# A four-layer kernel on one core: an input request moved ahead, a third buffer at the end, and a normalisation moved from VectorE to ScalarE

## The chip, the cores and the metric

The kernel runs on one core of a Trainium2 chip. The metric is device time in microseconds. The engines are TensorE (PE in the profile; its weight loads are PEld), VectorE (DVE), ScalarE (ACT), GpSimd (POOL) and SyncE (SP), which here only issues DMAs. Each engine runs its own instructions in order and waits on semaphores for others. A DMA is issued by an engine's queue and carried out by sixteen DMA engines.

## The reference

The input is x of shape (16, 192, 64, 64) in float32. Four layers follow, each of the form x = x + layer(group_norm(x)), with 32 groups:

- layer 0 passes each value, less and plus one half, through a small per-channel network of tanh and linear maps; the difference of two sigmoids is a likelihood.
- layer 1 is a 1x1 convolution over the image and its four shifts by one pixel.
- layer 2 is a selective scan. The image is read in four orders (by rows, by columns, and both backwards). For each order, channel and each of 16 states:

```
dA = exp(delta * A)
h  = dA * h + (delta * u) * B
y  = sum over the 16 states of h * C
```

- layer 3 sums four depthwise convolutions (3x3, 5x5, 1x7, 7x1), mixes channels by a 1x1 convolution z, normalises z over the whole batch and clips it to 0..6.

Since layer 3's statistics run over all 16 images, its last step can only be done when z is known for all of them.

## The kernel before, in words

Two images form a pair: 384 channels are three tiles of 128 partitions (NT = 3) with 4096 pixels. There are eight pairs. `front` computes layers 0 and 1 and layer 2's projections of a pair; `scans` computes layer 2; `layer3` the convolutions and z, which goes to memory. `pair` calls `scans` and `layer3` in turn. The front of the next pair is a Python generator that `scans` advances by pieces between its own steps, so that its work lies among the scan's on every engine. Only the first pair's front runs alone, and the last pair's scans have no front beside them.

**Scans.** For each tile j, each order k and each chunk m of 1024 pixels there is a block t (48 blocks), and in it one step for each of the 16 states n (768 steps s). A step has: a broadcast load cb of a row of C (SP, two steps ahead), `spread` of B by PE into PSUM (two steps ahead), `decay` (ACT exponent, three steps ahead), `product` (DVE), `scan` (DVE, then ACT copies the last column to `state`, then POOL multiplies h by cb; at n % 4 == 1 a POOL DMA adds the neighbour's h), and `add_up` by PE four steps later, which sums h in PSUM. There are eight h buffers. The scans' instructions go through `_Engines(tc, True)`, so they stay in program order; everything made with `_Engines(tc, False)` or with `nc` directly is placed by the planner, which takes an instruction when its inputs and buffers are free in its own account of time.

Once per block, `step_rest` makes the next block's delta (n == 4, with two table loads on ACT) and du (POOL; n == 8). Once per tile, `load_xn` requests the next tile of x at step 14 of the last block but one (block 14 or 30), and `norm_xn` normalises it at step 5 of the last block (15 or 31). There is one xn buffer, so the request waits until the last du has read it.

**Layer 3 and `begin`.** `begin` prepares the first block of the next pair: it loads xn, dt and bp, normalises xn on DVE, and makes delta and du. `layer3` calls it before its third quarter (c == 2).

**The end.** With the batch statistics loaded (zs) and turned into a scale and a shift, 24 tiles are read back (zl from SP, rl, the layer's own input, from ACT's queue), finished by one ACT and one DVE instruction of 4096 columns, and stored from SP. zl and rl have two buffers each.

Of the kernel before, what the change touches and what calls it, by code (L numbers as in the profile page):

```python
# [11 lines left out]
F32 = mybir.dt.float32  # L12
BF16 = mybir.dt.bfloat16
AF = mybir.ActivationFunctionType
# [8 lines left out]
P = 128  # L23
C = 192
NT = 3
# [11 lines left out]
K, N, R = 4, 16, 6  # L37
LC = 1024
# [68 lines left out]
def conv_preact_kernel(ctx: ExitStack, tc: tile.TileContext, a: dict):  # L107
# [737 lines left out]
        E.table(SOFTPLUS)  # L845
        E.act.activation(delta, v, AF.Softplus, bias=dtb[:, k, j : j + 1])

    def begin(o, psum):


        E = _Engines(tc, False)
        k = ORDER[0]
        xn = over.tile([P, L], F32, name="xn")
        nc.sync.dma_start(out=xn, in_=row_tiles(o.x2)[:, 0, :])
        dt = load_dt(nc.sync, o, k, 0)
        bp = load_bp(nc.sync, o, k, 0)
        normalise(nc.vector, xn, xn, o.gm, o.rstd, 0)
        delta = over.tile([P, LC], F32, name="delta", tag="delta", bufs=2)
        make_delta(E, psum(), delta, dt, k, 0)
        du = over.tile([P, LC], F32, name="du", tag="du", bufs=2)  # L860
        nc.gpsimd.tensor_tensor(image(du), image(delta), columns(xn)[:, : LC // HW, :], ALU.mult)
        return xn, bp, delta, du

    def scans(i, o, p3, st3, begun, nxt):

        E = _Engines(tc, True)
        with ExitStack() as es:
# [43 lines left out]
                    xns[j] = over.tile([P, L], F32, name="xn")  # L911
                    E.sp.dma_start(out=xns[j], in_=row_tiles(o.x2)[:, j, :])

            def norm_xn(j):
                if j < NT:
                    normalise(E.dve, xns[j], xns[j], o.gm, o.rstd, j)

            def load_xc(t):
                if t < T and todo[t][1] == 0:
# [148 lines left out]
            for s in range(total):  # L1068
                t, n = divmod(s, N)
                j, k, at, first = todo[t]  # L1070
                if s + 2 < total:
                    load_c(s + 2)
                if n == 2:
                    next_bp(t + 1)
                if n == 4:
                    next_dt(t + 2)
                if n == 6:
                    load_xc(t + 1)
                product(s)
                E.between()  # L1080
                scan(s)


                if n == 4:
                    gstep = step_rest(t + 1) if t + 1 < T else iter(())
                    next(gstep, None)
                if s + 3 < total:
                    decay(s + 3)
                if s + 2 < total:
                    spread(s + 2)  # L1090
                if (t + 2) % (K * NC_) == 0 and n == 14:
                    load_xn(j + 1)
                if (t + 1) % (K * NC_) == 0 and n == 5:
                    norm_xn(j + 1)
                if n > 4:
                    next(fin, None)
                if t == T - 1 and n > 2:
                    next(gn0, None)
                if n == 3:
                    add_up(s - LATE)  # L1100
                    if s >= LATE and (s - LATE + 1) % (K * NC_ * N) == 0:
                        fin = finish(j - 1)
                elif n == 8:
                    next(gstep, None)

                if kind == "l0":
                    for _ in range({5: 0}.get(n, 1)):
                        kind = next(fr, None) if kind == "l0" else kind
                elif n != 5:
                    done = 0  # L1110
                    while done < (1.99 if n in (0, 8, 12) else 0.99) and kind != "l0":
                        kind = next(fr, 1)
                        done += kind if isinstance(kind, float) else 1
                if n != 3:
                    add_up(s - LATE)
# [10 lines left out]
    def layer3(i, st3, less0, rstd0, o_next):  # L1126
        E = _Engines(tc, False)

        with tc.tile_pool(name="l3s", bufs=1) as stat, tc.tile_pool(name="l3z", bufs=2) as zk, tc.tile_pool(
# [14 lines left out]
                on_scalar(E, v, v, less0, rstd0, 0)  # L1144
            pw = load("pw", [P, len(BLOCKS), P], w_)
            nc.sync.dma_start(out=x3_d[i, NT - 1], in_=X)
            gm = stat.tile([P, NT], F32, name="gm")
            rstd = stat.tile([P, NT], F32, name="rstd")
            banks = lambda name: pz.tile([P, 512], F32, name=name, tag="ps")
# [13 lines left out]
            begun = None  # L1163
            for c in range(4):
                if c == 2 and o_next is not None:
                    begun = begin(o_next, lambda: pt.tile([P, 1024], F32, name="l3_p"))
                ys = []
                for j in range(NT):

                    g = wk.tile([P, 1024], F32, name="l3_g")  # L1170
                    for tap in TAPS[PE_TAPS:own]:
                        first = tap is TAPS[PE_TAPS]
                        m = g if first else wk.tile([P, 1024], F32, name="l3_m", bufs=3)
                        nc.scalar.activation(  # L1174
                            image(m), window(j, 16 * c, 16, tap), AF.Copy, scale=factor(j, tap)
                        )
                        if not first:
                            nc.gpsimd.tensor_tensor(g, g, m, ALU.add)  # L1178
                    ps = pt.tile([P, 1024], F32, name="l3_p")
                    for h in range(2):  # L1180
                        cs = slice(512 * h, 512 * h + 512)
                        for t, tap in enumerate(TAPS[:PE_TAPS]):
                            nc.tensor.matmul(  # L1183
                                ps[:, cs],
                                diag[:, j, t, :],
                                window(j, 16 * c + 8 * h, 8, tap),
                                start=(t == 0),
                                stop=False,
                            )
                    for half in range(2):  # L1190
                        for r in range(2):
                            rows = slice(64 * r, 64 * r + 64)
                            h = (half + r) % 2
                            cs = slice(512 * h, 512 * h + 512)
                            nc.tensor.matmul(  # L1195
                                ps[rows, cs], ident[rows, rows], g[rows, cs], start=False, stop=True
                            )

                    y = wk.tile([P, 1024], F32, name="l3_y", tag=f"l3_y{j}")
                    for tap in TAPS[own:]:  # L1200
                        nc.vector.scalar_tensor_tensor(  # L1201
                            image(y if tap is TAPS[-1] else ps),
                            window(j, 16 * c, 16, tap),
                            factor(j, tap),
                            image(ps),
                            ALU.mult,
                            ALU.add,
                        )
                    ys.append(y)
                for jo in range(NT):  # L1210
                    z = zk.tile([P, 1024], F32, name="z")
                    for h in range(2):
                        ps = pz.tile([P, 512], F32, name="zp", tag="ps")
                        for n, (b, ji) in enumerate(INTO[jo]):
                            nc.tensor.matmul(  # L1215
                                ps,
                                pw[:, b, :],
                                ys[ji][:, 512 * h : 512 * h + 512],
                                start=(n == 0),
                                stop=(n == len(INTO[jo]) - 1),  # L1220
                            )
                        nc.scalar.copy(z[:, 512 * h : 512 * h + 512], ps)
                        nc.vector.bn_stats(zst[:, jo, 2 * c + h, :], z[:, 512 * h : 512 * h + 512])
                    nc.sync.dma_start(
                        out=row_tiles(z_d[i])[:, jo, 1024 * c : 1024 * c + 1024], in_=z
                    )
# [15 lines left out]
        for _ in front(0, sets[0], _Engines(tc, False), Banks(ps, 8), True):  # L1242
            pass
    with tc.tile_pool(name="b_ps", bufs=1, space=PSUM) as ps:
        begun = begin(sets[0], lambda: ps.tile([P, LC], F32, name="b_v"))
    for i in range(npair):
        begun = pair(i, i % 2, i + 1 if i + 1 < npair else None, begun)

# [1 line left out]
    with tc.tile_pool(name="fin", bufs=1) as fin, tc.tile_pool(  # L1250
# [42 lines left out]
        nc.vector.tensor_tensor(shift, mean, scale, ALU.mult)  # L1293
        nc.vector.tensor_tensor(shift, beta, shift, ALU.subtract)

        with tc.tile_pool(name="last", bufs=2) as lp:
            for i in range(npair):
                for j in range(NT):
                    z = lp.tile([P, L], F32, name="zl")
                    r = lp.tile([P, S, S], F32, name="rl")  # L1300
                    nc.sync.dma_start(out=z, in_=row_tiles(z_d[i])[:, j, :])
                    nc.scalar.dma_start(out=r, in_=x3_d[i, j])
                    nc.scalar.activation(  # L1303
                        z, z, AF.Relu, bias=shift[:, j : j + 1], scale=scale[:, j : j + 1]
                    )
                    nc.vector.scalar_tensor_tensor(  # L1306
                        image(z), image(z), 6.0, r[:, inside, inside], ALU.min, ALU.add
                    )
                    nc.sync.dma_start(out=row_tiles(out[i])[:, j, :], in_=z)
# [107 lines left out]
```

## Time and profile before

| | us |
|---|---|
| median of 3 runs | 27652.14 (27644.76 to 27657.57) |
| profiled execution | 27649.24 |
| its span | 27647.5 |
| DVE busy | 23966.9 (87%) |
| PE busy | 23437.4 (85%) |
| POOL busy | 20728.4 (75%) |
| ACT busy | 16170.9 (58%) |

The first pair's scans lie between 1202 and 4120 us of the span, its layer 3 between 4120 and 4460; each later pair repeats this. The end begins at about 27180. Busy shares are averages over these unlike stages. Two helpers record most instructions under one line (L66 for all that is kept in order), so groups are told apart by the tiles that they write and read. "Idle before" in a group is the time in which the engine stood still just ahead of it, and the name after it is what ended that. Idle time of an engine that isn't the one others wait for costs nothing.

### The profile page before, as it was taken

To read this page: it belongs to the slowest core of one execution; us is meant where nothing else is said; L and a number is where in the kernel's file an instruction comes from. 1 tells how busy PE (TensorE), PEld (TensorE's weight loads), DVE (VectorE), ACT (ScalarE), POOL (GpSimd) and SP (SyncE) were. 2 spreads that over 40 slices of the span, in tenths; PEclk is the share of its full clock that TensorE was granted. 3 is DMA by queue.
4 is the path that set the end of the run, shared out by engine and by line. 5 is a ranking of instruction groups with operands and counts; after the bars stand their busy time and mean duration, and the time that the engine had idled before them with its cause. 6 is when DMAs were issued, how large, how long until landed. Compare 5 with 4: busy or idle time off the path is not lost. (4 is left out here: it accounts for less than half of the span.)

```text
span 27647.5 us, 208708 instructions
## 1 busy us (share of the span) xinstructions
PE 23437.4 (85%) x57652; PEld 9614.6 (35%) x57652; DVE 23966.9 (87%) x15146; ACT 16170.9 (58%) x23198; POOL 20728.4 (75%) x10386
## 2 busy tenths in 40 slices
PE   8799978999789987999779997899978998776672
PEld 4343323433233332433334332333323333222221
DVE  0399988999899998999989998899989999899994
ACT  7388455874468644885548844587447855444442
POOL 2388877887778876888768887788777887677771
PEclk9899989999899998999889998999989999888886
DMA  4489874898568973898748986589747897367755
GB/s 102 135 224 228 222 213 137 226 223 223 156 193 227 226 225 119 226 226 224 218 128 226 226 219 191 157 227 223 226 133 213 225 224 226 113 189 194 198 163 243
DMA packets 1999218, 5471.76 MB, mean 198 GB/s; under 512 B 550440, under 2 KB 550664, under 8 KB 1977568
## 3 DMA queue, kind: packets, MB, share of 16 engines
q1 hardware_dynamic: 1773408, 4592.80, 56.4%
q0 software_dynamic: 221184, 805.40, 15.3%
q10 hardware_dynamic: 3456, 60.21, 0.6%
q8 instruction: 459, 7.52, 0.1%
q14 instruction: 711, 5.82, 0.1%
HBM read 3908.47 MB, written 340.96 MB: 154 GB/s over the span
## 5 line engine op out<-in xcount | busy, mean ns | idle before, releaser
L66 POOL TENSOR_TENSOR h<-h,cb 128x1024 f32<-128x1024 f32 x6144 | 14878.4, 2479 | 4244.1 <-ACT state L66 3331.4
L66 DVE TENSOR_TENSOR_SCAN h<-dA,state,pbt 128x1024 f32<-128x1024 f32 x4608 | 10809.2, 2346 | 736.2 <-ACT dA L66 106.0
L66 PE MATMUL ysum<-h,ident 128*128 128x512 f32 x18432 | 9427.6, 637 | 191.3 <-DMA h<-h 188.6
L66 DVE TENSOR_TENSOR pbt<-du,pbt 128x1024 f32<-128x1024 f32 x6144 | 7427.4, 1209 | 592.2 <-PE pbt L66 444.7
L66 ACT ACTIVATE dA<-delta,t_alog 128x1024 f32<-128x1024 f32 x6144 | 7042.4, 1148 | 6.5
L66 PEld LDWEIGHTS ysum<-h,ident 128*128 128x128 f32 x18432 | 3765.1, 205 | 4487.1 <-issue 3914.3
L66 ACT COPY state<-h 128x1 f32<-128x1 f32 x6144 | 1144.3, 186 | 6214.0 <-DVE h L66 6193.5
L66 PE MATMUL pbt<-bp,pick 96*128 96x512 bf16 x8192 | 2695.6, 414 | 1929.7 <-DVE h L66 1917.8
L66 DVE TENSOR_TENSOR_SCAN h<-dA,pbt 128x1024 f32<-128x1024 f32 x1536 | 3507.8, 2284 | 203.1 <-ACT dA L66 33.1
L66 PE MATMUL p<-t,wts 96*128 96x512 f32 x5376 | 2688.7, 598 | 122.0 <-ACT t L66 121.5
L66 PE MATMUL p<-m,wms 128*96 128x512 f32 (+1 forms) x5376 | 2658.9, 596 | 9.0 <-ACT t L66 5.3
L66 ACT ACTIVATE t<-p,bias 96x512 f32<-96x512 f32 x2688 | 1803.1, 678 | 914.5 <-PE p L66 901.9
L66 PEld LDWEIGHTS <-pick 96*128 96x128 bf16 x8192 | 697.3, 101 | 4716.9 <-DVE h L66 3101.5
L1178 POOL TENSOR_TENSOR l_g<-l_g,l_m 128x1024 f32<-128x1024 f32 x672 | 1614.5, 2404 | 633.5 <-ACT l_g L1174 455.6
L66 PE MATMUL l_p<-l_xp,w1s 128*128 128x512 f32 x3920 | 1840.3, 598 | 17.0 <-POOL l_xp L66 17.0
L66 PE MATMUL pbt<-bp,pick_mix 96*128 96x512 bf16 x4096 | 1283.6, 396 | 541.6 <-DVE h L66 535.7
L66 POOL DMA_DIRECT2D h<-h x1536 | 1365.5, 889 | 495.9 <-POOL h L66 421.5
L66 PEld LDWEIGHTS p<-t,wts 96*128 96x128 f32 x5376 | 1010.7, 190 | 1259.2 <-issue 890.5
L66 ACT ACT_TABLE_LOAD x1082 | 1388.2, 1283 | 19.2
L66 PEld LDWEIGHTS p<-m,wms 128*96 128x96 f32 (+1 forms) x5376 | 946.8, 177 | 746.3 <-issue 363.8
L1201 DVE SCALAR_TENSOR_TENSOR l_p<-xp,wc,l_p 128x1024 f32<-128x1024 f32 x768 | 985.6, 1289 | 244.5 <-PE l_p L1195 220.7
L66 ACT ACTIVATE m<-m,bias,sp 96x512 f32<-96x512 f32 x1344 | 1078.0, 803 | 174.0 <-DMA m<-l_xn 157.9
(242 smaller groups left out, 18743.2 us busy)
## 6 DMA issues: line engine op xcount, KB each, us to landing
cb<-cp_d SPq DMA_DIRECT2D x2048, 512.0 KB
cb<-c_d SPq DMA_DIRECT2D x2048, 512.0 KB
h<-h POOLq DMA_DIRECT2D x1536, 512.0 KB, 7.0
cb<-cp_d SPq DMA_DIRECT2D x2048, 256.0 KB
cb<-c_d SPq DMA_DIRECT2D x2048, 256.0 KB
m<-l_xn SPq DMA_DIRECT2D x3072, 128.0 KB
bp<-bp_d SPq DMA_DIRECT2D x384, 192.0 KB
x_d<-X SPq DMA_DIRECT2D x24, 2450.0 KB
```

The costliest lines, as they stand in the source:

```text
L66: return self._tc.keep_in_program_order(call(*args, **kw))
L1178: nc.gpsimd.tensor_tensor(g, g, m, ALU.add)
L1201: nc.vector.scalar_tensor_tensor(image(y if tap is TAPS[-1] else ps), window(j, 16 * c, 16, tap), factor(j, tap), image(ps), ALU.mult, ALU ...
```

## The change

Five edits in three parts:

- The three loads of `begin` become `load_first`, which `layer3` calls at its start, after it has requested its own inputs; `begin` takes the loaded tiles. For the first pair `load_first` is called right before `begin`.
- `norm_xn` in the scans no longer runs as one DVE instruction of 4096 columns, but as four parts of 1024 at steps 5 to 8, each of two ACT instructions (`on_scalar`: add the negative mean, multiply by the inverse deviation). `less`, the negative mean, is computed once per pair on ACT. Since du of the next tile's first block reads all four parts, `next(gstep)` for du goes from n == 8 to n == 10, in every block.
- The pool `last` has three buffers in place of two.

```diff
-    def begin(o, psum):
-        E = _Engines(tc, False)
+    def load_first(o):
         k = ORDER[0]
         xn = over.tile([P, L], F32, name="xn")
         nc.sync.dma_start(out=xn, in_=row_tiles(o.x2)[:, 0, :])
         dt = load_dt(nc.sync, o, k, 0)
-        bp = load_bp(nc.sync, o, k, 0)
+        return xn, load_bp(nc.sync, o, k, 0), dt
+
+    def begin(o, loaded, psum):
+        E = _Engines(tc, False)
+        k = ORDER[0]
+        xn, bp, dt = loaded
         normalise(nc.vector, xn, xn, o.gm, o.rstd, 0)
...
+            less = p3.tile([P, NT], F32, name="less")
+            E.act.activation(less, o.gm, AF.Copy, scale=-1.0)
+
-            def norm_xn(j):
+            def norm_xn(j, part):
                 if j < NT:
-                    normalise(E.dve, xns[j], xns[j], o.gm, o.rstd, j)
+                    v = xns[j][:, LC * part : LC * part + LC]
+                    on_scalar(E, v, v, less, o.rstd, j)
...
-                if (t + 1) % (K * NC_) == 0 and n == 5:
-                    norm_xn(j + 1)
+                if (t + 1) % (K * NC_) == 0 and 5 <= n < 5 + NC_:
+                    norm_xn(j + 1, n - 5)
...
-                elif n == 8:
+                elif n == 10:
                     next(gstep, None)
...
             nc.sync.dma_start(out=x3_d[i, NT - 1], in_=X)
+            loaded = load_first(o_next) if o_next is not None else None
...
-                    begun = begin(o_next, lambda: pt.tile([P, 1024], F32, name="l3_p"))
+                    begun = begin(o_next, loaded, lambda: pt.tile([P, 1024], F32, name="l3_p"))
...
-        with tc.tile_pool(name="last", bufs=2) as lp:
+        with tc.tile_pool(name="last", bufs=3) as lp:
```

## The prediction

> **What bounds the kernel now.** I read the busy time by stage first, since one average over 27.6 ms hides where each edit works. The columns are the stretch, its length, busy us of PE, weight loads, DVE, ACT and POOL, then the granted clock, the DMA share and GB/s. The rows are: the scans of the first pair, its step block 15, its step block 31, its layer 3, and the end.
>
> ```profile
> 1202.00:4120.00 2918.00, 2601.85 (x6544) 1071.65 (x6544) 2733.79 (x1662) 1883.11 (x2776) 2379.97 (x1209) 0.94 0.83 223
> 2060.00:2120.00 60.00, 58.24 (x151) 24.12 (x150) 56.04 (x34) 49.12 (x73) 49.31 (x27) 1.00 0.88 250
> 3060.00:3120.00 60.00, 58.50 (x153) 25.14 (x152) 58.30 (x38) 23.25 (x34) 47.59 (x24) 1.00 0.95 240
> 4120.00:4460.00 340.00, 277.25 (x641) 113.67 (x640) 241.59 (x207) 128.36 (x125) 207.88 (x87) 0.88 0.08 31
> 27180.00:27647.50 467.50, 7.94 (x36) 7.83 (x36) 107.91 (x35) 91.09 (x24) 0.86 (x1) 0.50 0.85 346
> ```
>
> In the scans DVE is busy 94% (2733.79 of 2918), PE 89%: DVE sets the step, about 3.6 us of it (scan 2.35, product 1.21). The last stage is another kernel: DMA at 0.85, every engine nearly idle.
>
> Then the chain that ended last, for one round of the end (start, us, what), and the timeline of the first round:
>
> ```profile
> 27564.73 19.23 DMA out<-zl
> 27584.03 9.73 DMA zl<-z_d
> 27593.83 3.81 ACT zl L1303
> 27597.66 4.44 DVE zl L1306
> 27602.12 19.68 DMA out<-zl
> ...
> 27203.26 0.20 DVE L1269 TENSOR_REDUCE acc<-zs 128x3 f32<-128x24 f32 x1 [21.65 <-DMA zs<-zstat_d]
> ...
> 27222.81 4.67 SPq L1309 DMA_DIRECT2D out<-zl  x2
> 27222.82 4.69 ACTq L1302 DMA_DIRECT2D rl<-x_d  x2
> 27236.29 11.01 SPq L1301 DMA_DIRECT2D zl<-z_d  x2
> ```
>
> Two tiles go round together: two stores, two loads behind them, both engines, 37.5 us per two tiles (27227.15 to 27639.9 in eleven rounds). The second store and the load after it are DMA time; ACT and DVE of the second tile (8.2 us) are time with nothing queued. Two short stretches show it, one in that hole, one in the loads:
>
> ```profile
> 27257.00:27260.00 3.00, 0.00 (x0) 0.00 (x0) 3.00 (x1) 3.00 (x1) 0.00 (x0) 0.50 0.00 0
> 27285.00:27293.00 8.00, 0.00 (x0) 0.00 (x0) 0.00 (x0) 3.57 (x1) 0.00 (x0) 0.50 0.99 426
> ```
>
> Last, what the moved work costs now, from the groups and the issues of the next pair's first input on SP:
>
> ```profile
> L66 DVE TENSOR_SCALAR xn<-xn,gm,rstd 128x4096 f32<-128x4096 f32 x16 | 45.6, 2849 | 0.0
> L346 ACT ACTIVATE xp<-xp,first 128x1024 f32<-128x1024 f32 x32 | 37.1, 1158 | 0.0
> L66 POOL TENSOR_TENSOR du<-delta,xn 128x1024 f32<-128x1024 f32 x376 | 1022.3, 2719 | 0.0
> ...
> 4021.82 0.80 SPq L832 DMA_DIRECT2D dt<-dtp_d  x2
> 4038.18 0.32 SPq L854 DMA_DIRECT2D xn<-x_d  x1
> 4054.22 0.42 SPq L825 DMA_DIRECT2D bp<-bp_d  x1
> ```
>
> **What the Trainium skill says.** "Perfetto Trace Analysis", Identifying Performance Opportunities (Optimization Strategy): the same gap repeating on the resource that should be saturated can mean too few buffers for the next tile. The hole of every round fits. "DMA: Bandwidth & Descriptors", Where 436 GB/s comes from: a ceiling of 435 GB/s for the ports, and some 358 where HBM takes part. Full stretches here, all from or to HBM, show 426 to 432: the first agrees, the second doesn't bind this core. Same page, Queues, rings and completion order: each DMA engine alternates between queues packet by packet, so a small-packet transfer on one queue waits for large packets on another. The trace agrees: the statistics (zs, 24-byte packets) take until 27203 behind two rl tiles. "ScalarE: Activation LUTs", Table sets: copy and identity lie in every table set; in layer 3's on_scalar group no table load appears.
>
> **The change, part by part**, against the profiled execution (27649.24 us, span 27647.5; the median shown, 27652.14, lies 2.9 above it).
>
> *The input request.* xn was written at layer 3's third quarter, but the planner already issues it at 4038, while the scans run to 4120, as soon as the last du (4035.79 to 4038.15 on POOL) releases the buffer. dt and bp go at 4022 and 4054. Asking earlier in the program can't come before that release. All four DMA issues (two dt, xn, bp; 1.5 us of SP) lie in the same place on SP, ahead of layer 3's stores. Worth 0. If the cover were gone, a 14 us load (4038 to the normalise at 4052.21) per pair would be exposed, 7 x 14 = 98 us; nothing removes it: du is two steps (7 us) later, and the scans have 82 us to go. The normalise in begin remains on DVE. That layer 3, freely planned, is reordered I price at -10 to +20.
>
> *Three buffers at the end.* A tile moves 2048 + 2450 + 2048 KB = 6.70 MB; at 432 GB/s that is 15.5 us. Two tiles: 31.0 of the 37.5 us, so 6.5 us of hole and ramp per round. With three tiles in flight, the first of the next three loads has landed, and ACT and DVE (8.2 us) run, while two loads of 4.9 us (9.8) are still moving: the hole shrinks to a ramp of some 1.7 us (the first store is issued at 27260.3, full rate comes near 27262). Round of three: 46.5 + 1.7 = 48.2. Now: last store minus first store is 417.1 (27222.8 to 27639.9). After: seven rounds of 48.2 = 337.4, plus two spacings of 4.9 = 347.2. Against it: a third rl tile (2.5 MB) goes ahead on the ACT queue, and zs, on whose arrival everything waits, is passed by it: 2.5 MB at the 344 GB/s that queue had there = 7.3 us later. Net 417.1 - 347.2 - 7.3 = -62.6. Bounds: DMA without any ramp from the start gives -77; the hole staying at 6.5 per round of three gives 52.9 x 7 + 9.8 + 7.3 = 387.4, or -30.
>
> *Normalisation on ScalarE.* Removed: 16 DVE instructions, 45.6 us, in a stage that DVE paces. Added: 16 x 4 parts x 2 activations of 1.158 us = 148 us of ACT, 9.3 per tile at steps 5 to 8, and one tiny activation per pair. In block 31 ACT is busy 23 of 60 us: hidden, and the whole DVE time returns (eight tiles, 25.2 us by the single instructions). In block 15 layer 0 of the next pair runs: ACT 49 of 60, with two table loads just before, at step 4. Queued behind the parts are the copy of the state (POOL's multiply waits for it), the decay three steps ahead (about 7 us of lead over the scan), and layer 0's tanh, for which PE waits, and behind PE the spread that DVE needs. Four steps then hold 0.19 + 1.15 + 2.3 + 1.4 to 2.1 = 5.0 to 5.7 us of ACT against 3.6: some 7 us of backlog, of which 3.5 to 7 is lead. I take a stall of 2.5 us, as much as the removed 2.4 to 2.7: zero for seven pairs. The last pair has no front beside it: 2.4. Sum -25 after PE takes some (98% busy in block 31). Bounds: all returns, -46; the stall is 7 us, +5.
>
> *du two steps later*, in all 376 cases. It now runs before step 9's multiply and its accumulating DMA; PE's wait for such a DMA is worst for step 9 (88 of 189 us, sorting those waits by the step's number). Later, it lies three steps ahead of the next such DMA (step 13). Its own reader, the next block's first product, is five steps off. I take -8; bounds -40 and +20 (all such waits of DVE and PE, 119 and 189, are the stock).
>
> Sum: 0 - 62.6 - 25 - 8 = -95.6; 27649 - 96 + 3 = 27557.
>
> **Rivals.**
> 1. *ACT gives back what DVE saves, or du's shift nothing* (chance 0.2): block 15 stalls 5 to 7 us in seven pairs, PE at 97% takes the rest. For it: ACT 82% there; against: block 31 is free. Sum -62 + 10 = about 27600.
> 2. *The end hardly gains* (0.12): the transfer volume sets it, and zs comes still later because the third zl is also ahead of it. For it: the share is 0.85 already. -30 at the end, -25 elsewhere: 27597; with nothing elsewhere 27622.
> 3. *Slower* (0.08): du in its new place makes step 13's multiply late, its DMA lands later, and the scan four to five steps on, at step 2 of the next block, finds no free h buffer (eight of them). du costs 2.72 us; if 0.5 us of it reaches DVE in each of 376 blocks, that is +188, less the gains of 62 and 25: 27753. It decides from (62 + 25 + 55) / 376 = 0.38 us per block. Against it: POOL is busy 82%, and at step 14, the same place in today's order, DVE waits only 50 us in all for these DMAs.
> 4. *The request was late after all and its move helps*: excluded by 4038.18 above; 0.
>
> **How the numbers follow.** The main case has 0.6, with its own range 27525 to 27595. All three others lie above it; below it only the bounds (-77, -46, -40). 27510 to 27635 leaves 0.08 above (rival 3) and about 0.1 below and between. A difference of 0.2%, 55 us, is about what this kernel's measurement can tell: faster means under 27597. Nearly all of the main case (0.57), half of rival 1 and a part of rival 2 are faster: 0.72; the rest of these is the same, 0.2; slower 0.08.
>
> **What would show it.** The end: rounds of three stores, 16.1 us per tile, DMA share near 0.95; zs landing some 7 us later after the stage's first load than the 22 us of now. Scans: sixteen tensor_scalar gone from DVE; block 31 shorter by about 3 us, block 15 the same; waits of DVE for dA up at steps 9 to 12 of block 15. du: PE's wait for h<-h down at step 9. Layer 3: 340 us as before, xn issued some 7 us nearer the scans' end. I am wrong if the end's rounds stay above 17.5 us per tile, if blocks other than 15 and 31 change by over 0.3 us each, or if layer 3's length moves.

## The result and the profile after

The changed kernel takes 27583.09 us (median of nine runs, 27559.04 to 27592.56) beside 27647.85 for the kernel before; the ratio is 0.9975 with a 95% interval of 0.9965 to 0.9985. The forecast was 27557 with a range of 27510 to 27635. The profiled execution has a span of 27590.8 us, 56.7 less than the one before (27647.5).

These are the stages of the changed kernel: the first pair's scans, block 15 and block 31 of the second pair (from the first scan of the block to the first scan of the next), the first layer 3, and the end (stretch, length, PE, weight loads, DVE, ACT, POOL, clock, DMA share, GB/s).

```profile
1201.30:4136.70 2935.40, 2617.68 (x6544) 1078.54 (x6544) 2730.40 (x1660) 1898.93 (x2791) 2376.90 (x1208) 0.94 0.83 222
5371.00:5438.00 67.00, 59.00 (x145) 24.12 (x144) 56.56 (x34) 56.40 (x79) 52.25 (x27) 0.95 0.80 228
6346.70:6407.50 60.80, 60.80 (x160) 26.58 (x159) 59.04 (x38) 32.74 (x45) 51.40 (x27) 1.00 0.99 247
4136.70:4476.10 339.40, 279.22 (x640) 114.33 (x640) 241.67 (x209) 128.47 (x126) 207.86 (x87) 0.88 0.08 31
27199.00:27590.80 391.80, 7.94 (x36) 7.82 (x36) 107.83 (x36) 90.98 (x24) 0.86 (x1) 0.50 0.98 413
```

The same two blocks of the second pair in the kernel before:

```profile
5361.10:5422.20 61.10, 57.21 (x146) 23.91 (x145) 58.35 (x35) 48.30 (x72) 51.12 (x27) 0.97 0.86 246
6334.30:6398.70 64.40, 62.05 (x163) 26.81 (x162) 62.65 (x39) 24.41 (x37) 53.39 (x27) 1.00 0.93 239
```

Four things are to be seen. Block 31 got shorter, from 64.4 us to 60.8, and block 15 longer, from 61.1 to 67.0. The end shrank from 467.9 us (from the last statistics of z) to 391.7, and its DMA share rose from 0.85 to 0.98. And the first pair's scans did not get shorter, though DVE lost work: 2935 us in place of 2918.

The scans are laid out alike in every pair, so they can be compared block by block: the time from the first scan of a block to the first scan of the next, summed over the eight pairs, after minus before. Two runs below that touch nothing in the scans show sums of up to 10 us for one block from chance alone, most under 5.

| place | us, eight pairs |
|---|---|
| the end | -76.1 |
| blocks 5 and 6 | -41.8 |
| blocks 22 and 23 | -14.2 |
| block 15 | +29.3 |
| blocks 16 and 17 | +12.7 |
| block 31 | -25.5 |
| block 32 | -12.6 |
| block 33 | +62.0 |
| all other blocks together | +12.6 |
| layer 3, eight times | -2.3 |
| first front and rest | -0.8 |

In these two executions the scans as a whole cost 22.5 us more. That total by itself can be chance: in the two runs that leave the scans alone it came out at -9.8 and +33.7. By the medians the whole change is worth -64.8 us, beside -76.1 at the end, so the scans gave nothing and may have cost some 11. The end pays for everything. The chain that ended last, at the end of the changed kernel (start, us, what):

```profile
27427.44 18.43 DMA out<-zl
27445.94 19.84 DMA zl<-z_d
27465.85 3.81 ACT zl L1313
27469.68 4.44 DVE zl L1316
27474.14 19.31 DMA out<-zl
```

One turn of a buffer now takes 46.7 us, but three tiles share it: 15.6 us per tile where two shared 37.5, 18.7 per tile. While the 8.2 us of ACT and DVE pass for one tile, the other two keep the DMAs full. The timeline of the first rounds shows why the start didn't get later either:

```profile
27202.72 0.66 SPq L1267 DMA_DIRECT2D zs<-zstat_d  x1
...
27222.85 0.19 DVE L1279 TENSOR_REDUCE acc<-zs 128x3 f32<-128x24 f32 x1 [21.86 <-DMA zs<-zstat_d]
27234.12 3.80 ACT L1313 ACTIVATE zl<-zl,shift,scale 128x4096 f32<-128x4096 f32 x1 [36.24 <-DVE shift L1304]
27234.12 0.33 ACTq L1312 DMA_DIRECT2D rl<-x_d  x1
```

The third rl tile is requested on ACT's queue behind the first activation, at 27234, not ahead of zs. zs arrives 20.1 us after its request, before 19.8.

The next pair's first input xn is asked for at 4062, 75 us before the first pair's scans end (at 4137). In the kernel before it was asked for at 4038, 82 us before their end (at 4120). In the changed kernel:

```profile
4038.16 0.80 SPq L832 DMA_DIRECT2D dt<-dtp_d  x2
4062.05 0.32 SPq L853 DMA_DIRECT2D xn<-x_d  x1
4074.60 0.72 SPq L825 DMA_DIRECT2D bp<-bp_d  x1
```

### The profile page after: what moved, and what is told of

Its sections match the earlier page's. It is cut to its first block, busy times and chain, and to the rows that moved or that the text cites. A ratio compares the mean times of both kernels' runs of the same rounds, so it can differ in the third digit from the quotient of the medians.

```text
span 27590.8 us, 208880 instructions
## 1 busy us (share of the span) xinstructions
PE 23489.0 (85%) x57652; PEld 9644.7 (35%) x57652; DVE 23927.1 (87%) x15130; ACT 16294.9 (59%) x23334; POOL 20702.8 (75%) x10386
## 5 line engine op out<-in xcount | busy, mean ns | idle before, releaser
L66 PE MATMUL l_p<-l_xp,w1s 128*128 128x512 f32 x3920 | 1848.0, 600 | 14.4 <-POOL l_xp L66 14.4
```

Source lines behind the costliest of these rows:

```text
L66: return self._tc.keep_in_program_order(call(*args, **kw))
```

## The experiments

The theory to be tested: the parts add up; the end is all of the gain; du's shift makes blocks 5, 6, 22 and 23 shorter and block 33 longer; the normalisation on ScalarE is what makes block 15 longer. Rivals are named with each run. Ratios are to the kernel before, measured again beside the runs: 27656.01 us for the first four, 27645.57 for the later ones. Sums over blocks are taken from one profiled execution of each run, after minus before.

### The three buffers alone

```diff
-        with tc.tile_pool(name="last", bufs=2) as lp:
+        with tc.tile_pool(name="last", bufs=3) as lp:
```

> The kernel before with three buffers in the last pool, nothing else. Theory (the parts add up, and the end is freed from its hole): the end, from the last statistics of z to the end of the span, goes from 467.9 to about 392 us, all scans stay as before; total -76 us, 27572. Rival (part of the end's gain in the full change came from elsewhere, such as an earlier start of its loads): the end gains under 60 us here.

Measured: 27585.89 us beside 27656.01, ratio 0.9972 (0.9962 to 0.9983). The end takes 391.8 us:

```profile
27168.20:27560.00 391.80, 7.94 (x36) 7.83 (x36) 107.83 (x36) 90.98 (x24) 0.86 (x1) 0.50 0.98 413
```

The rival falls. One line of the change gives as much as the whole of it.

### The early request alone

The edits of `load_first` and `begin`, with the pool, the normalisation and du as before.

> The early request alone. Theory (the planner had issued it at the release of xn already): no difference, within 10 us; xn is issued some 80 us before the scans end, layer 3 stays at 340 us. Rival (the request reorders layer 3 or SP's queue and is what makes block 33 longer in the full change): block 33 grows by about 9 us in seven pairs, +60 us.

Measured: 27658.77 beside 27656.01, ratio 1.0001 (0.9992 to 1.0010); layer 3 is unchanged (0.0 us over eight), block 33 too (+0.6). The request does nothing, and the rival falls.

### du at step 10 alone

```diff
-                elif n == 8:
+                elif n == 10:
                     next(gstep, None)
```

> du at step 10 in place of step 8 alone. Theory (du's shift is the cause both of the shorter blocks 5 and 6 and of the longer block 33, where a later POOL makes the accumulating DMA of block 32's step 13 land behind the store of X): blocks 5 and 6 -42 us over eight pairs, block 33 +50 to +62, blocks 22 and 23 -10; total +5 to +20 us. Rival (block 33 grows because DVE runs ahead after the normalisation has left block 31): block 33 as before, total about -50 us.

Measured: 27640.1 beside 27656.01, ratio 0.9996 (0.9987 to 1.0005). By blocks: 5 and 6 -37.2, 22 and 23 -14.1, 32 -19.6, 33 +64.4. So block 33 belongs to du's shift and not to the normalisation, and so do the gains in the other blocks. They cancel: a run that can't be told from the kernel before holds 71 us of gain and 64 of loss. Block 32's part I had put down to the normalisation.

The gain in blocks 5 and 6 is the step-9 accumulating DMA leaving earlier: 9.4 to 9.5 us after its scan in place of 12.1. Over the eight pairs the scans of these two blocks waited 41.7 us for it before and 0.9 in this run. DVE's waits in the two blocks of the second pair, before and then in this run, where none for a DMA is left (waiting and waited for: us, times, longest):

```profile
DVE h L66 <- DMA h<-h: 5.5, 2, 3.4
DVE pbt L66 <- PE pbt L66: 2.4, 2, 1.4
DVE h L66 <- DVE pbt L66: 0.6, 3, 0.2
DVE h L66 <- POOL h L66: 0.2, 1, 0.2
```

```profile
DVE pbt L66 <- PE pbt L66: 2.4, 2, 1.4
DVE h L66 <- DVE pbt L66: 1.2, 6, 0.2
```

PE waits less for such DMAs too. Over the whole kernel, before and in this run:

```profile
PE ysum L66 <- DMA h<-h: 188.6, 100, 9.1
PE ysum L66 <- DMA h<-h: 140.5, 73, 7.7
```

In block 23 the scans wait for the DMA of step 5 and not of step 9 (14.0 us before, 7.3 here). How du's new place brings that about is not shown.

The loss has one place. Here is the end of block 32 in the second pair before (POOL issues the accumulating DMA of step 13, SP the store of the finished tile X):

```profile
6462.78 0.87 POOL L66 DMA_DIRECT2D h<-h  x1 [0.30 <-POOL h L66]
6465.99 0.71 SPq L66 DMA_DIRECT2D x_d<-X  x1
```

and in this run, with the scan of step 1 in block 33:

```profile
6458.20 0.87 POOL L66 DMA_DIRECT2D h<-h  x1 [0.30 <-POOL h L66]
6458.30 0.42 SPq L66 DMA_DIRECT2D x_d<-X  x1
6472.86 2.35 DVE L66 TENSOR_TENSOR_SCAN h<-dA,state,pbt 128x1024 f32<-128x1024 f32 x1 [10.20 <-DMA h<-h]
```

In block 32 POOL also adds the column-wise sums of the finished tile to the row-wise ones (four additions of about 3.1 us at steps 5 to 11). du now stands among the last of these, the step-13 multiply comes later against its scan, and its DMA starts within 0.1 us of the 2450 KB store in place of 3.2 us ahead of it. In the changed kernel it lands 14.9 us after its issue, before 6.6. The scan of the next block that needs its buffer waits 10.2 us. The store's packets are of 19600 bytes, the accumulating DMA's of 4096; the Trainium skill, "DMA: Bandwidth & Descriptors", Queues, rings and completion order, has each DMA engine take turns between queues by whole packets, which would give the store the larger share. That fits, but is no proof: a packet of that page groups several descriptors, and the rows counted here need not be packets in its sense. Whether the store or POOL's lag does it is not decided by this run.

Two other places help. The last pair has no front beside it, and its DMA in block 32 left within 0.1 us of the store in the kernel before already. It took 14.5 us there too, with POOL no later than in the changed kernel (10.5 us after the scan in both):

```profile
25979.90 14.52 DMA h<-h
```

Block 16 has the same additions and a store of the same size, and POOL's lag grows there as well, from 13.4 to 16.2 us in most pairs. But in six of the seven pairs with a front the DMA leaves 4 to 6 us ahead of the store there, lands in about 7 us, and no scan waits. In the fourth pair the two leave 0.6 us apart; there the DMA takes 13.6 us and a scan waits 4.8.

### The store of X later

The changed kernel, with the store moved from step 15 of block 32 to step 7 of block 33 (the expectation says step 8; three more turns of the generator end at step 7). The store in block 16 moves in the same way.

```diff
                     yield
+                for _ in range(3):
+                    yield
                 if j < NT - 1:
                     E.sp.dma_start(out=x3_d[i, j], in_=X)
```

> The whole change, but the store of X to memory that follows a tile's last sum is issued three steps of the generator later (step 2 after 5 of the next block at the earliest: at its step 8 in place of step 15 of the block before). Theory (block 33 waits because the accumulating DMA of block 32's step 13 now lands behind this 2450 KB store): block 33 gives back its 62 us, total about 27583 - 60 = 27523; that DMA lands in 6 to 9 us. Rival (POOL being two steps later in block 32 is enough by itself): block 33 stays within 10 us of the changed kernel's.

Measured: 27557.95 beside 27645.57, ratio 0.9965 (0.9952 to 0.9979). Block 33 is +30.0 in place of +62.0: neither expectation. The wait at its step 1 is halved, with the store gone from there:

```profile
6457.96 0.87 POOL L66 DMA_DIRECT2D h<-h  x1 [0.30 <-POOL h L66]
6467.16 2.35 DVE L66 TENSOR_TENSOR_SCAN h<-dA,state,pbt 128x1024 f32<-128x1024 f32 x1 [4.78 <-DMA h<-h]
```

The DMA lands in 9.1 us. Means over the seven pairs with a front (us) separate the causes:

| | DMA issued after its scan began | lands in | scan of step 1 waits |
|---|---|---|---|
| before | 9.5 | 6.9 | 0.6 |
| changed kernel | 11.5 | 14.4 | 9.9 |
| store later | 11.6 | 8.5 | 4.2 |

Of the 9.3 us that the changed kernel waits longer, some 2 are POOL's lag and some 6 go with the store. The other 1.6 remain when the store is gone: the later DMA lands more slowly, and with what other traffic it then competes is open. In the last pair, where POOL's lag is the same in all kernels, moving the store alone takes the landing from 13.8 to 7.5 us. And the moved store delays the DMA of block 33's step 5 in its turn: 2.2 us per pair at step 10. So both causes are there, the store's the larger.

### The normalisation on ScalarE alone

The edits of `less`, `norm_xn` and its call, with du at step 8.

> The normalisation on ScalarE alone, du at step 8. Theory: block 15 with its next two +42 us over the pairs with a front (ACT's backlog delays layer 0's tanh, PE waits for it, and the spread comes late), -2.4 in the last pair; blocks 31 and 32 -38; block 33 as before; total about +2 us. Rival for block 33 (DVE ahead): +62 there, total about +65. Rival for block 15 (du at step 10 is what stalls it): block 15 about 0 to -2 us per pair, total about -40.

Measured: 27686.32 beside 27656.01, ratio 1.0010 (1.0003 to 1.0017): this part alone makes the kernel 30 us slower. Blocks 15 to 17 +38.6, of which the last pair, with no front, has -2.4 in block 15; block 33 -1.8; blocks 31 and 32 only -3.0, where the changed kernel has -38. Part of that difference is du's -20 in block 32. The remainder, block 31's -7.4 against -25.5, goes with du being at step 8, where it must wait for the last part on ACT; DVE then waits 1.4 us per pair for PE at step 8. What joins the two was not tried.

In block 15 of the second pair PE's waits in the kernel before and, below it, in the changed kernel are (waiting and waited for: us, times, longest):

```profile
PE pbt L66 <- DVE h L66: 2.2, 2, 1.9
PE p L66 <- ACT t L66: 1.7, 1, 1.7
```

```profile
PE p L66 <- ACT t L66: 8.0, 3, 3.2
```

t is layer 0's tanh. It stands on ACT behind the normalisation's parts; PE, in order, waits for it, and the spread of B that the scan's product needs stands behind that on PE. The sums over block 15 of all pairs follow this chain: PE's wait for t is 8.8 us before, 43.7 in this run and 48.3 in the changed kernel; DVE's wait for the spread is none before, 43.8 and 51.2 us.

### Layer 0 not advanced beside the parts

```diff
-                    for _ in range({5: 0}.get(n, 1)):
+                    for _ in range(0 if n == 5 or (t == K * NC_ - 1 and 5 < n < 9) else 1):
```

> The whole change, but layer 0 of the next pair isn't advanced beside the parts of block 15 (steps 6 to 8; step 5 skips it already). Theory (layer 0's tanh stands behind the parts on ACT, PE waits for it, and the spread of B waits behind PE): PE's wait for t in block 15 falls from 8 to about 2 us per pair, block 15 shrinks by 29 to 45 us over the pairs, blocks 16 and 17 by up to 10; the three steps are made up later at no cost, total about 27545. Rival (the parts delay the copy of the state and the decay themselves, whoever else is on ACT): block 15 as in the changed kernel.

Measured: 27626.11 beside 27645.57, ratio 0.9993 (0.9984 to 1.0001). Block 15 goes from +29.3 to -19.7, so that the whole DVE time comes back in each pair (-1.5 to -3.1), and in the same block PE no longer waits for t:

```profile
PE pbt L66 <- DVE h L66: 5.5, 3, 3.0
```

Over all pairs DVE's wait for the spread in block 15 falls from 51.2 to 3.0 us. The rival falls: the parts by themselves hold up neither the copies nor the decays. The block has also lost three steps of layer 0's work on PE (54.1 us busy in place of 59.0 in the second pair), so its length alone would not tell whose queue mattered; the waits do. The other half of my expectation falls as well. The run is some 43 us slower than the changed kernel: with layer 0 three steps later, what follows meets other steps, and blocks 31 and 32 are 37 and 50 us longer than in the changed kernel. The front's steps were not spare. Which meeting costs this is open.

### What cost time taken out

```diff
-                if (t + 1) % (K * NC_) == 0 and 5 <= n < 5 + NC_:
+                if t + 1 == K * NC_ and nxt is not None:
+                    if n == 5:
+                        norm_whole(j + 1)
+                elif (t + 1) % (K * NC_) == 0 and 5 <= n < 5 + NC_:
                     norm_xn(j + 1, n - 5)
...
-                elif n == 10:
+                elif n == (8 if t > 0 and t % (K * NC_) == 0 else 10):
                     next(gstep, None)
```

`norm_whole` is the single DVE instruction of before.

> The change without what cost time: the second tile (block 15) is normalised on DVE again where a front runs beside it, and du is made at step 8 in blocks 16 and 32, at step 10 elsewhere. Theory (the parts add up): end -76, blocks 5 and 6 -40, 22 and 23 -14, block 31 about -20, blocks 15 to 17 and 33 as in the kernel before; about -150, 27506. Rival (blocks that get shorter give it back in the next ones, since PE is nearly full beside layers 0 and 1): -110 or less.

Measured: 27490.18 beside 27645.57, ratio 0.9944 (0.9928 to 0.9961): faster than both kernels, by 155 us than before. The end -76.5, blocks 5 and 6 -39.5, 22 and 23 -14.8, 31 -26.4; block 15 -5.4 and block 33 -5.0, back to where they were. DVE's waits for the accumulating DMAs in the whole kernel, before, in the changed kernel and in this run, show the gain without the loss:

```profile
DVE h L66 <- DMA h<-h: 118.8, 73, 4.6
DVE h L66 <- DMA h<-h: 127.1, 52, 10.3
DVE h L66 <- DMA h<-h: 55.5, 46, 4.8
```

The parts add up: -155 by the medians where -150 was expected.

### The later store in place of the earlier du

As the last one, with du at step 10 in every block and the store of X as in the run with the later store.

> The same with du at step 10 in every block and the store of X later instead. Theory: as the one before, with block 32's -20 kept as well if the store is what holds block 33: about -165, 27490. Rival (POOL's lag by itself): block 33 +60, about 27550.

Measured: 27524.14 beside 27645.57, ratio 0.9956 (0.9941 to 0.9971). Block 32 keeps -13.8, but block 33 has +28.1, as with the later store before: about half-way between the two expectations. Putting du back where POOL is crowded is the better cure, by 34 us.

## Why the prediction was right or wrong

*The request: right.* It was priced at 0 because the planner had issued xn at the release of its buffer; alone it gives 1.0001, and layer 3 keeps its 340 us.

*The end: right in kind, too small in size.* -62.6 forecast, -76.1 measured, next to the bound of -77. Two terms of the sum were wrong. The 7.3 us for zs did not come (the first store leaves 43.4 us after the last statistics, before 43.2): the step assumed that the third rl is issued together with the first two, but it stands behind an activation on ACT's own queue. Its price was unsupported as well: the trace has 277 GB/s for the first two rl tiles and not 344, and zs stood behind a zl tile on its own queue too, so what held it back is not shown. And the 1.7 us of ramp per round did not come (340.9 us from the first store to the last, where 347.2 was forecast): the step assumed rounds of three stores with a common hole, but stores and loads come apart (SP mostly issues them singly or in twos after the start), so that the share is 0.98 over the whole stretch.

*ScalarE: block 31 right, block 15 wrong.* The 25.2 us of block 31 came (-25.5), but only with the new place of du beside it; alone the move gave -7.4 there. For block 15 I wrote "I take a stall of 2.5 us, as much as the removed 2.4 to 2.7: zero for seven pairs". Seven pairs came out at +31.7 and the last at -2.4: 4.5 us per pair net, so a stall of about 7, the upper bound I had named. I also had the way of it wrong: DVE did not wait for dA at steps 9 to 12 (0.4 us in block 15 over all pairs), and the decays have three steps of lead. It waited for PE's spread, 2.1 and 2.2 us per pair at steps 10 and 12 and 1.9 at step 0 of the next block. PE's dependence on tanh has no such lead, and I had listed it third.

*du: near in sum, by luck.* -8 forecast. Alone it measures -16 by medians, with an interval that includes no change, and its blocks hold -71 and +64: a small sum because two larger terms, neither of them forecast at its size, cancel. The gain by the step-9 DMA was named and undersized. The loss is the mechanism of rival 3 (a later multiply, a later DMA, a scan without a buffer), but not spread over 376 blocks: it is in one block of each pair with a front, where POOL has extra additions and a large store shares the DMAs. "Its own reader, the next block's first product, is five steps off" looked at the wrong follower.

*The sum*: -62.6 - 25 - 8 against, in the two profiled executions, -76.1 at the end and +22.5 in the scans (some +11 by the medians). The total lay inside the range, even that of the main case, but the main case with its 33 us of gain in the scans did not come true: it is rival 1, at the end's full gain. That the number was so near is in part luck, since the end's surplus of 13.5 us made up for part of what the scans did not give. "I am wrong if blocks other than 15 and 31 change by over 0.3 us each" did apply, to blocks 5, 6, 23, 32 and 33 (chance alone can reach 1.3 us per block, so that 0.3 was too fine a sign).

## What to carry to other kernels

In a ring of buffers around a nearly saturated DMA, look for a hole in the DMA share that repeats in every round: here one more slot covered the compute between a load and its store, and the hole and ramp of 6.5 us times eleven or twelve rounds (72 to 78 us) was about the gain (76). An instruction moved to an engine with idle time can cost what is queued behind it: look for the follower with the shortest lead, not the one named first. And an instruction moved in every iteration must be checked in the iterations that have something extra; a neutral total can hide a gain and a loss of the same size.

## What the runs showed of the hardware

Small and large transfers in flight together share the DMAs badly for the small one: the 512 KB accumulating DMA took 6.6 us when it left 3.2 us before the 2450 KB store, and 14.9 us when both left within 0.1 us. In the last pair, with POOL equally late, it took 14.5 and 13.8 us (before and in the changed kernel) with the store beside it, and 7.5 with the store moved away. In the end's stage, reads and writes of device memory together held 413 GB/s over 391.8 us.
